# Moving the second group of row constants from the last y blocks to the place behind the first group

## The chip, the cores and the metric

The kernel runs on one NeuronCore of a Trainium2 chip. The metric is the device time of one execution in microseconds, the median over runs. The engines meant below are TensorE (PE; its weight loads are PEld), VectorE (DVE), ScalarE (ACT), GpSimd (POOL) and SyncE (SP). POOL and SP issue the DMA transfers: SP the plain ones, POOL the gathers and scatters by row number.

## The reference

The input is a matrix x of 2708 rows by 1024 columns and a 0/1 adjacency matrix of 2708 by 2708 with few ones in most rows. Two layers follow each other; each ends in a layernorm over the row.

```
q, k, v = x @ Wq.T + bq, x @ Wk.T + bk, x @ Wv.T + bv
z = (q @ k.T) / 32 * adj;  z = where(z == 0, -10000, z)
x1 = layernorm(x + relu(softmax(z, axis=1) @ v))
out = layernorm(x1 + adj @ (x1 @ W1) + b1)
```

Where a row of the adjacency matrix has any ones, only the columns with a one carry weight in the softmax. The kernel uses that: for each row it lists the columns with a one and works on those alone. A dense version follows in the program and is entered only if a check on the data fails.

## The kernel before, in words

The rows are handled in 22 blocks of 128 (`NB`; the last has 20 rows). Four pieces of work matter here.

**The y rows.** The score of rows i and j is rewritten as y_i . x_j plus a constant of row i, with y = x M + a bias row, and M made once from Wq and Wk. `y_block(b)` computes the block of y for the b-th 128 rows of x: two halves of 512 columns, each a chain of matmuls into one PSUM bank (L319), an add of the bias row by DVE that empties the bank (L323, raised in priority), and a write of the block to DRAM on SP's queue (L328). The next x block is loaded, transposed, on SP's queue (L280, three buffers `xt`). Along with it ACT sums the columns of x (L332).

**The row constants.** `row_constants(f)` makes the constant of each row, a dot product of the row of x with a vector `u_bc`. For each block it loads 128 rows of x into a tile `g` (L681, 512 KB, SP's queue), multiplies and sums in one DVE pass (L682), and at the end adds one number (L683) and writes the constants behind the y rows in DRAM (L684). Family 0 is row blocks 0 to 7 (eight passes), family 1 is blocks 8 to 20 (thirteen passes). The tiles `g` come from a pool of nine buffers (`G1 = 9`), which the attention gathers use as well, in the order in which they are asked for.

**The records.** Rows are sorted by their number of ones, and a record for each (its columns, its row number) is scattered to DRAM by POOL (L563) and read back into `tabs` (L568). `records_back(1, put)` turns the second family's records into masks on DVE (L593, L581, L582); its first step is told to stand behind `put`, the last DVE step of `row_constants(0)`.

**Attention and projection.** In the sorted order, a job of `attend` gathers 128 rows of y (`yg`, L343, two buffers) and for each slot 128 rows of x (`g`, L349), all on POOL's queue; takes a score for each slot with a DVE pass (L813, with L820 and L840 behind it), the exponentials on ACT (L849, L868) and sums the weighted rows with further DVE passes (L870) into `r`. Two jobs with many slots are worked in another form (`attend_shares`, L947). `flip` transposes `r` on PE (L716), ACT copies it out (L717) and `project` multiplies it by Wv (L739). `finish0` adds the bias (L906) and the gathered x row `xr`, and normalizes. The projection shares the four PSUM banks `po` with the y blocks.

The order is written out by hand: `steps` lists the y blocks 8 to 21 ("y"), the projections ("v") and later pairs of them ("p"), and a running credit decides in which step a job is started. Row blocks of records with family 1 can start only when all of y is written. A scheduler puts the instructions of each engine into one queue according to this order, their priorities and their dependences. [...]

In the kernel before, `row_constants(1)` is called in that loop, just ahead of `y_block(17)` (`b == NB - 5`), when family 1's y rows are still being computed.

Of the kernel before, what the change touches and what calls it, by code (L numbers as in the profile page):

```python
# [80 lines left out]
def sparse_part(ctx, tc, x, xT, adj, wqT, wkT, wvT, bq, bk, bv, w1, b1, out):  # L81
# [5 lines left out]
    NB = (N + P - 1) // P  # L87
# [23 lines left out]
    with es:  # L111
# [224 lines left out]
        def follow(later, earlier, same=False):  # L336

            kind = mybir.DependencyClass.NoSync if same else mybir.DependencyClass.Sync
            tc.add_manual_dep(later.ins, earlier.ins.name, mybir.DependencyInfo(kind, mybir.DependencyReason.DATA),
                              reason="an engine's queue shall not stand still for a transfer")  # L340
# [235 lines left out]
        def masks(ok, less_, d):  # L576

            shape = list(ok.shape)
            of = [places[:, :shape[-1]], d.to_broadcast(shape)] if len(shape) == 2 else \
                [places[:, :shape[2]].unsqueeze(1).to_broadcast(shape), d.unsqueeze(2).to_broadcast(shape)]  # L580
            put = nc.vector.tensor_tensor(ok, *of, op=ALU.is_lt)  # L581
            nc.vector.tensor_scalar(less_, ok, FAR, -FAR, op0=ALU.mult, op1=ALU.add)  # L582
            return put

        def records_back(f, behind=None):
            b0, nb = families[f]
            bs, js = slice(b0, b0 + nb), slice(0, max(SLOTS[max(b0, 1):b0 + nb]))
            if f == 0:
                deg0 = lists.tile([P, 1], F32, name="deg0")
                follow(nc.vector.tensor_copy(deg0, tab0[:, DEG:DEG + 1]), products[-1])  # L590
                nc.vector.tensor_scalar_add(deg0[:HUB], deg0[:HUB], float(-J0))
                masks(valid0, less0, deg0)
            put = nc.vector.tensor_copy(degs[:, bs], tabs[:, bs, DEG])  # L593
            follow(put, products[-1] if behind is None else behind, same=behind is not None)
            masks(valid[:, bs, js], less[:, bs, js], degs[:, bs])
# [69 lines left out]
        def g_tile():  # L665

            return gp.tile([P, D], F32, name="g", tag="g")
# [9 lines left out]
        def row_constants(f):  # L677
            b0, end = families[f][0], min(sum(families[f]), NB - 1)
            for b in range(b0, end):
                xg = g_tile()  # L680
                nc.sync.dma_start(out=xg, in_=x[b * P:(b + 1) * P])  # L681
                nc.vector.scalar_tensor_tensor(junkv, xg, 1.0, u_bc, op0=ALU.mult, op1=ALU.mult, accum_out=c_all[:, b, 0:1])  # L682
            put = nc.vector.tensor_scalar(c_all[:, b0:end, 0], c_all[:, b0:end, 0], y_bc[:, D:D + 1], None, op0=ALU.add)  # L683
            nc.sync.dma_start(out=y_ds[f][:(end - b0) * P, D:].rearrange("(b p) e -> p b e", p=P), in_=c_all[:, b0:end])  # L684
            return put

        put = row_constants(0)
        records_back(1, put)

        def gather(src, b, word, n):  # L690
            return gather_slot(src, tabs[:n, b, word:word + 1], n, g_tile())

        def gather_x(src, b):

            xr = wp.tile([P, D], F32, name="xr", bufs=3)
            return gather_at(src, tabs[:rows[b], b, ROW:ROW + 1], rows[b], xr)
# [280 lines left out]
        def turn_pair(flips, pool):  # L977

            A = []
            for k, flip_to in enumerate(flips):  # L980
                rT = (pool if k else wp).tile([P, DC, P], F32, name="rT", bufs=2)
                A.append(flip_to(rT))
            if len(flips) == 1:
                return A, None
            (a11, a12), (a21, a22) = [(a[:, :DC // 2], a[:, DC // 2:]) for a in A]
            s_all = wm_pool.tile([P, 4, DC // 2, P], F32, name="s_all", tag="m3")
            S = [s_all[:, i] for i in range(4)]
            nc.vector.tensor_add(S[0], a21, a22)
            nc.vector.tensor_sub(S[1], S[0], a11)
            nc.vector.tensor_sub(S[2], a11, a21)  # L990
            halves_turned.append(nc.vector.tensor_sub(S[3], a12, S[1]))
            return A, S

        def differences():
            return [wm_pool.tile([P, DC // 2, HALF], F32, name=f"t{k}", tag=f"m{k - 2}") for k in (2, 3, 4)]
# [97 lines left out]
        def blocks_of(step):  # L1093
            return [] if step[0] == "y" else [step[1]] if step[0] == "v" else list(step[1])
# [4 lines left out]
        def run_job():  # L1099

            b = jobs.pop(0)
            if b not in running:
                running[b] = (attend_one if b in single else attend_shares if b in (0, "hub") else attend)(b, got)
            next(running[b])
            J = HUB_SLOTS if b == "hub" else SLOTS[b]
            return 1.6 if b in single else SMALL + SLOT * J / len(pieces(J))

        def turn0(b):
            if b in last:
                rT = hp.tile([P, DC, HUB], F32, name="mean", tag="y0T")  # L1110
                nc.scalar.copy(rT, xbT.unsqueeze(2).to_broadcast([P, DC, HUB]))
                return rT
            return flip_shares([got["hub"], got[0]]) if b == 0 else flip(got[b])
# [5 lines left out]
        for i, (kind, b) in enumerate(steps):  # L1119
            if pending is not None:  # L1120
                pending[0](*pending[1:])
                credit -= END * (2 if pending[0] is finish_pair else 1)
                pending = None
            credit += STEP if kind != "p" else 2 * STEP - P_END
            step[0] = i
            for entry in joining[:]:
                if i >= entry[1] + 2:
                    entry[1] = i
                    next(running[entry[0]])
                    if entry[0] in got:  # L1130
                        joining.remove(entry)
            if kind == "p" and b == pairs[0]:

                (q11, q12), (q21, q22) = wv_q
                wv_t = differences()
                nc.vector.tensor_sub(q12, q12, q11)
                nc.vector.tensor_sub(wv_t[0], q22, q12)
                nc.vector.tensor_sub(wv_t[1], wv_t[0], q11)
                nc.vector.tensor_sub(wv_t[2], q21, wv_t[0])
            for c in [c for st in steps[i:i + 3] for c in blocks_of(st) if not (left_y and c in late)]:  # L1140
                while c not in done0 and c not in got and c != 0:
                    credit -= run_job()
            while 0 in jobs and i >= 15:
                credit -= run_job()
            while jobs and credit > 0 and len([c for c in got if c not in done0 and c not in ALONE and c != "hub"]) < (RB - 1 if left_y else RB):
                if left_y and len(jobs) <= late_jobs:
                    break
                credit -= run_job()
            for k, c in steps[i:i + 2]:
                if k != "y" and c not in turned and not (left_y and k == "p"):  # L1150
                    turned[c] = turn0(c) if k == "v" else turn_pair([lambda rT, r=got[b_]: flip(r, rT) for b_ in c], xb_pools[0])
                    done0.update(blocks_of((k, c)))
            if kind == "y":
                if b == NB - 5:
                    row_constants(1)
                y_block(b)
                credit -= Y_END
                left_y -= 1
                if left_y == 0:
                    xa.release()  # L1160
                    xb_pool = tc.alloc_tile_pool(name="xb", bufs=1, side="right", reuse_waits="tile")
                    xb_pools.append(xb_pool)
                    xb_bc.append(xb_pool.tile([P, D], F32, name="xb_bc"))
                    bcast_rows(xb_bc[0], xbT)
            elif kind == "v":
                xr = gather_x(x, b)
                pending = finish0, b, (project_mean if b in last else project)(turned[b], wv_q), xr
            else:
                for b_ in b:
                    pair_x[b_] = gather_x(x, b_)  # L1170
                pending = finish_pair, b, project_pair(b, *turned[b])
# [472 lines left out]
```

## Time and profile before

| | |
|---|---|
| median of 3 runs | 1066.83 us (1064.39, 1066.83, 1071.95) |
| profiled execution, span from first to last instruction | 1065.8 us |
| profiled execution, its own device time | not printed beside the span |
| PE busy | 1007.5 us (95%) |
| DVE busy | 850.6 us (80%) |
| POOL busy | 493.0 us (46%) |
| L682, one pass | 1.218 us median, 21 passes, from 250.5 to 486.7 us |
| L681, one load | 512 KB, 8.0 us median to landing |
| L349 gather of 128 rows of x | 1.0 us on POOL, 5.5 us median to landing |

A line of the profile's timeline gives the start in microseconds from the first instruction, the length, the engine, the line of the program, the operation, and what is written and read; in brackets stands how long the engine had been idle before it and whose event ended that. A line by stretch gives the busy time of each engine in it.

### The profile page before, as it was taken

How to read it: one execution, taken by the hardware profiler on the slowest of the kernel's cores; microseconds unless marked ns; L12 is line 12 of the kernel's file. 1: busy time of each engine (PE TensorE's matmuls, PEld its weight loads, DVE VectorE, ACT ScalarE, POOL GpSimd, SP SyncE). 2: the span in 40 equal slices, each digit the busy share in tenths (PEclk: the TensorE clock that was granted, in tenths of full speed). 3: DMA queues.
4: the chain of work that ended last, by engine and by line, in shares of the span. 5: the costliest groups of instructions: out<-in, count | busy, mean ns of one | idle time of the engine just before them, and what ended most of it. 6: DMA issues, size and time to landing. Idle time of an engine off the chain costs nothing.

```text
span 1065.8 us, 10216 instructions
## 1 busy us (share of the span) xinstructions
PE 1007.5 (95%) x2849; PEld 475.1 (45%) x2849; DVE 850.6 (80%) x1831; ACT 425.4 (40%) x894; POOL 493.0 (46%) x397
## 2 busy tenths in 40 slices
PE   7999999999988999999999999999589999999993
PEld 6444444444443444444545444444334444454441
DVE  8799999995287879999399999974678878896432
ACT  4688788422042332224424344332422363333321
POOL 1000140057654545526166666611577777787300
PEclk9999999999999999999999999999799999999997
DMA  9555458565887656796533777726589689979701
GB/s 363 184 205 204 167 207 290 160 216 168 292 250 253 200 181 203 236 331 201 175 114 96 239 247 258 260 95 210 151 286 262 201 274 324 282 221 323 192 40 42
DMA packets 90963, 229.20 MB, mean 215 GB/s; under 512 B 18411, under 2 KB 40395, under 8 KB 88189
## 3 DMA queue, kind: packets, MB, share of 16 engines
q0 software_dynamic: 48768, 148.05, 43.5%
q1 hardware_dynamic: 42128, 80.41, 21.9%
q8 instruction: 24, 0.39, 0.2%
q14 instruction: 43, 0.34, 0.1%
HBM read 219.61 MB, written 33.68 MB: 238 GB/s over the span
## 4 chain that ended last, share of the span: by engine, by line
PE 24%; DVE 12%; issue 5%; DMA 5%; POOL 3%; ACT 1%; POOLq 0%; DVEq 0%; ACTq 0%
PE po L999 21%; DVE r L870 3%; DMA g<-x_d,tabs 3%; DVE junkv L813 3%; DVE t L1011 1%; DMA yg<-y_d,tabs 1%; POOL g L349 1%; POOL xr L343 1%; PE tr L716 1%; PE po L739 1%; PE tr L729 1%; ACT junks L775 1%; DVE t L1069 1%; DVE r L1241 1%; DMA out_dram<-xr,tabs 0%
## 5 line engine op out<-in xcount | busy, mean ns | idle before, releaser
L319 PE MATMUL po<-m_sb,xt 128*128 128x512 f32 x672 | 292.1, 593 | 3.9 <-DVE yo L323 3.9
L319 PEld LDWEIGHTS po<-m_sb,xt 128*128 128x128 f32 x672 | 126.4, 190 | 160.1 <-issue 151.9
L813 DVE SCALAR_TENSOR_TENSOR junkv<-yg,g 128x1024 uint8<-128x1024 f32 x109 | 133.0, 1220 | 34.1 <-DMA g<-in_x_dram,tabs 16.7
L349 POOL DMA_INDIRECT g<-in_x_dram,tabs x86 | 110.7, 1288 | 72.3 <-DVE r L870 20.4
L999 PE MATMUL po<-t,s_all 128*128 128x512 f32 x272 | 124.3, 600 | 2.7 <-DVE xr L1011 2.7
L1241 DVE SCALAR_TENSOR_TENSOR r<-g,valid,r 128x1024 f32<-128x1024 f32 x77 | 98.6, 1281 | 19.1 <-DMA g<-x_d,tabs 18.3
L609 PE MATMUL po<-wk_o,wq_o 128*128 128x512 f32 x256 | 110.5, 592 | 0.0
L739 PE MATMUL po<-wv,rT 128*128 128x512 f32 x224 | 99.4, 602 | 3.6 <-DVE pr L855 3.0
L775 ACT ACTIVATE junks<-t,lnm 128x1024 uint8<-128x1024 f32 (+1 forms) x41 | 47.0, 1147 | 123.7 <-DVE lnm L773 95.2
L349 POOL DMA_INDIRECT g<-x_d,tabs x67 | 77.6, 1158 | 22.7 <-issue 12.8
L563 POOL DMA_INDIRECT tab_d<-rec,pos_i x22 | 27.1, 1230 | 130.0 <-DVE pos_i L552 123.6
L870 DVE SCALAR_TENSOR_TENSOR r<-g,pr,r 128x1024 f32<-128x1024 f32 x64 | 81.8, 1279 | 5.9 <-ACT r L882 4.6
L999 PE MATMUL po<-w,rT 128*128 128x512 f32 x192 | 86.4, 599 | 0.0
L332 ACT ACTIVATE junka<-xt 128x128 f32<-128x128 f32 x176 | 53.8, 306 | 76.1 <-PE po L319 57.5
L999 PEld LDWEIGHTS po<-t,s_all 128*128 128x128 f32 x272 | 51.9, 192 | 68.5 <-issue 61.9
L788 ACT ACTIVATE t<-t,nmr,rstd 128x1024 f32<-128x1024 f32 (+1 forms) x41 | 50.0, 1237 | 81.2 <-DVE nmr L787 81.0
L224 DVE MAX8 few<-a 128x8 f32<-128x75 f32 (+3 forms) x132 | 79.2, 618 | 0.0
L609 PEld LDWEIGHTS po<-wk_o,wq_o 128*128 128x128 f32 x256 | 48.3, 190 | 59.3 <-issue 59.1
L999 PE MATMUL po<-w,s_all 128*128 128x512 f32 x160 | 72.1, 592 | 0.0
L221 DVE SCALAR_TENSOR_TENSOR a<-a,iota 128x2708 f32<-128x2708 f32 (+1 forms) x22 | 65.2, 2963 | 5.4 <-ACT junk L220 5.4
L739 PEld LDWEIGHTS po<-wv,rT 128*128 128x128 f32 x224 | 42.8, 193 | 57.6 <-issue 56.8
L717 ACT COPY rT<-tr 128x512 f32<-128x512 f32 x80 | 43.1, 586 | 56.1 <-PE tr L716 56.1
(350 smaller groups left out, 1524.6 us busy)
## 6 DMA issues: line engine op xcount, KB each, us to landing
a<-in_adj_dram SPq DMA_DIRECT2D x21, 1354.0 KB, 5.9
xt<-in_xT_dram SPq DMA_DIRECT2D x21, 512.0 KB, 5.2
y_d<-yo SPq DMA_DIRECT2D x21, 512.0 KB, 6.1
g<-in_x_dram SPq DMA_DIRECT2D x21, 512.0 KB, 8.0
wq_i<-in_wqT_dram SPq DMA_DIRECT2D x8, 512.0 KB, 8.7
wk_i<-in_wkT_dram SPq DMA_DIRECT2D x8, 512.0 KB, 10.9
wv<-in_wvT_dram SPq DMA_DIRECT2D x16, 256.0 KB, 6.0
w<-in_w_dram SPq DMA_DIRECT2D x4, 1024.0 KB, 7.8
```

The costliest lines, as they stand in the source:

```text
L221: nc.vector.scalar_tensor_tensor(a[:n], a[:n], 1.0, iota[:n], op0=ALU.is_equal, op1=ALU.mult)
L224: nc.vector.max(few[:n, i * 8:(i + 1) * 8], a[:n, cuts[i]:cuts[i + 1]])
L319: put = nc.tensor.matmul(po, xt[:, c, :], m_sb[c // 2][:, c % 2, k0:k1], start=(c == 0), stop=(c == DC - 1))
L332: put = nc.scalar.activation(junka, xts[b][:, c, :], AF.Copy, accum_out=xs[:, c, b:b + 1])
L349: nc.gpsimd.indirect_dma_start(out=dst[:n], out_offset=None, in_=src, in_offset=bass.IndirectOffsetOnAxis(ap=at, axis=0), bounds_check=N - ...
L609: nc.tensor.matmul(po, wq_o[i // 2][:, o, i % 2 * P:(i % 2 + 1) * P], wk_o[:, o, hs], start=(o == 0), stop=(o == DC - 1))
L739: put = nc.tensor.matmul(acc, rT[:, c, :], w[c // 4][h][:, c % 4, :], start=(c == 0), stop=(c == DC - 1))
L775: nc.scalar.activation(junks[:n], t[:n], AF.Square, bias=nm[:n], accum_out=vs[:n])
L813: nc.vector.scalar_tensor_tensor(junkv[:n], yg[:n, :D], scale, xg[:n], op0=ALU.mult, op1=ALU.mult, accum_out=s)
L870: nc.vector.scalar_tensor_tensor(r[:n], xg[j][:n], pr[:n, j:j + 1], r[:n], op0=ALU.mult, op1=ALU.add)
L999: put = nc.tensor.matmul(acc, a[:, k], w[:, k], start=start and k == 0, stop=stop and k == DC // 2 - 1, skip_group_check=True)
L1241: put = nc.vector.scalar_tensor_tensor(r[:n], xg[:n], ok[:n, j:j + 1], r[:n], op0=ALU.mult, op1=ALU.add)
```

## The change

The call `row_constants(1)` is taken out of the loop over the steps and put directly behind `row_constants(0)` and `records_back(1, put)`, ahead of all attention jobs. It issues the same instructions: thirteen loads on SP's queue, thirteen DVE passes, one DVE add and one write. The thirteen tiles `g` are now asked for ahead of those of the first attention job. Lines behind the new call have a number that is one higher in the changed kernel up to the loop.

```diff
         put = row_constants(0)
         records_back(1, put)
+        row_constants(1)
...
             if kind == "y":
-                if b == NB - 5:
-                    row_constants(1)
                 y_block(b)
                 credit -= Y_END
                 left_y -= 1
```

## The prediction

> **What bounds the kernel now.** I read the page's busy shares first, then the busy time by stretch, then the queues of the vector engine (DVE) and of TensorE (PE) in order of time around the two places that the change touches, then PE's waits.
>
> ```profile
> span 1065.8 us, 10216 instructions
> PE 1007.5 (95%) x2849; PEld 475.1 (45%) x2849; DVE 850.6 (80%) x1831; ACT 425.4 (40%) x894; POOL 493.0 (46%) x397
> ```
>
> PE is busy 95%, so the 58 us in which it stands still are where time can be won or lost. By stretch (columns: length, then busy time of PE, PEld, DVE, ACT and POOL, clock, DMA share, GB/s), the place that the work leaves:
>
> ```profile
> 440.00:480.00 40.00, 40.00 (x95) 17.73 (x94) 38.66 (x64) 8.64 (x33) 14.18 (x11) 1.00 0.82 286
> 480.00:520.00 40.00, 40.00 (x152) 18.14 (x151) 31.35 (x68) 14.34 (x64) 18.40 (x15) 1.00 0.66 209
> ```
>
> PE has no gap there, though DVE is full until 510. The place that the work goes to is DVE's queue between 261 and 288:
>
> ```profile
> 261.62 0.23 DVE L683 TENSOR_SCALAR c_all<-c_all,y_bc 128x8 f32<-128x8 f32 x1
> 274.32 0.23 DVE L593 CAST degs<-tabs 128x14 f32<-128x14 int32 x1 [12.46 <-DMA tabs<-tab_d]
> 275.50 0.68 DVE L323 TENSOR_TENSOR yo<-po,y_bc 128x512 f32<-128x512 f32 x1
> 287.58 1.23 DVE L813 SCALAR_TENSOR_TENSOR junkv<-yg,g 128x1024 uint8<-128x1024 f32 x1 [11.41 <-DMA yg<-y_d,tabs]
> ```
>
> Two holes: 12.5 us until the second family's records are back, 11.4 us until the first row of y is gathered for attention. Behind the second, PE pays, because the adds that empty its four PSUM banks (L323) queue behind attention:
>
> ```profile
> 293.47 7.13 PE L319 MATMUL po<-m_sb,xt 128*128 128x512 f32 x16 [1.44 <-DVE yo L323]
> 301.55 7.13 PE L319 MATMUL po<-m_sb,xt 128*128 128x512 f32 x16 [0.95 <-DVE yo L323]
> 309.22 7.13 PE L319 MATMUL po<-m_sb,xt 128*128 128x512 f32 x16 [0.53 <-DVE yo L323]
> 318.16 14.04 PE L319 MATMUL po<-m_sb,xt 128*128 128x512 f32 x32 [0.93 <-DVE yo L323]
> 335.23 10.09 PE L739 MATMUL po<-wv,rT 128*128 128x512 f32 x19 [3.03 <-DVE pr L855]
> ```
>
> Together 6.9 us of PE stall. After 335 PE does not stop again until 524. The last y block ends at 523; its write and the late attention jobs hang on that, so whatever PE is early or late at 523 reaches the end of the kernel one for one.
>
> [...] the add of 292.73 stood behind the wait of 11.4 us although its matmuls had ended near 271 (halves of 6.9 us, counted back from 292.0). [...] L682 has a median of 1.218 us here.
>
> **The change, part by part.**
>
> *Removed at 453 to 488.* Thirteen L682 passes at a pitch of 1.27 us (253.55, 254.81, 256.08 in the first group) are 16.5 us of DVE, with 13 loads of 512 KB, one small add and one small write on SP. Direct worth: nothing, as PE covers it (80.0 of 80 us busy). DVE simply reaches its idle time earlier; from 509 to 523 it already stands still but for a few adds, waiting for PE and for a write of y. In the new order attention scores stand where the first L682 stood, so the adds near 464 are not freed; the relief starts near 478.
>
> *Added after 274.* In the built order of the changed kernel the copy of the records (L593) stays ahead of the 13 passes, so the first hole stays and only the second is used. Records arrive at 273.1 (the tabs load is issued 1.2 us earlier on POOL, since one gather no longer stands ahead of it). Then 13 x 1.27 = 16.5, the masks 1.2 and the two adds of block 8 1.2 us: DVE is free at 273.1 + 18.9, about 292.3 with the small add. Attention begins 292.5 against 287.6: it is 4.9 us late.
>
> *Moved on POOL.* In the built order the three xr gathers and the first two yg gathers come ahead of all g gathers. These g gathers need the buffers of the 5th to 13th pass: 281, 283, 284 and so on, with 6 us to land. The first three are there by 290, before DVE is free. From then on gather and pass form one loop over nine buffers (a pass frees a buffer, a gather of about 6 us fills it), which in the kernel before cost DVE 8.6 us of waiting from 300 to 345. I walked it pass by pass with 1.27 us passes and 6 us gathers. The waits come again: the first scores of row blocks 4, 3 and 2 start at 304.8, 317.6 and 333.7 against 299.7, 311.7 and 327.5, and block 2's last maximum is taken at 358.4 against 353.2. So the lag, call it d, is 5.2.
>
> *Moved on SP.* Five loads stand ahead of one xt load, seven ahead of the next; the seven wait for the first passes, so that xt goes out near 280 and not 271.5. It is used near 299: covered by some 14 us. If that cover is gone, PE waits for it.
>
> *What PE gains first.* The adds now stand ahead of attention or early in it. Block 8's second half is added at 287 (before 292.7), block 9's halves at 294 and 302 (before 300.8 and 308.5), block 11's at 324 and 333.6. PE needs those banks at 292, 299, 306, 327 and 334. All are in time, so the 6.9 us of stalls go.
>
> *What is late next.* PE is now up to 6.9 us early and DVE d late, and the banks' slack between them is finite. In the kernel before, the tightest are those of block 17:
>
> ```profile
> 457.26 0.68 DVE L323 TENSOR_TENSOR yo<-po,y_bc 128x512 f32<-128x512 f32 x1
> 464.20 0.68 DVE L323 TENSOR_TENSOR yo<-po,y_bc 128x512 f32<-128x512 f32 x1
> 464.10 13.90 PE L319 MATMUL po<-m_sb,xt 128*128 128x512 f32 x32
> ```
>
> The first bank is free at 457.9 and taken at 464.1, the second at 464.8 and 471.0: slack 6.2 both times (others have 7.1 to 13). PE can therefore be early by 6.2 - d at most, and every further microsecond of d makes it late. DVE does not wait for PE between 345 and 460, so nothing there works d off.
>
> *How large d is.* With 5.2 the gain is 1.0 us. Two things add to it that the trace does not price. Eight of the 13 loads (4.2 MB) now go out at 251 to 263, together with the 14 scatters of the records and ahead of their reading back; the DMA shares there are 0.72, 0.29, 0.62 and 0.17 per 5 us, so at some 400 GB/s (measured 285 to 290) the 10.5 us of traffic just fit, but a scatter or the reading back can be 0 to 5 us later. I take 2. And the scores that replace L682 near 464 need gathered rows: 0 to 2, I take 0.5. So d = 7.7 and the loss is 1.5 us. Bounds: d = 0 if the loop's waits swallow the lag (gain 6.2); d = 17 if DVE's hole is of no use (loss 10.8).
>
> The sum: 1065.8 + 1.5 in the span. The page prints no other time of that execution; its span is 1.0 below the median of the three runs, so I add the 1.5 to the median 1066.8: **1068.3 us**.
>
> **Rivals.**
> - *A, forecast:* the lag and the slack nearly cancel, d from 4.5 to 10: 1065 to 1071. [...] Chance 0.55.
> - *B, the lag is absorbed:* the waits for gathers in the kernel before (3.2 us at 332 and 365, 4.1 at 381) would be shorter when DVE comes later; with d of 0 to 2 PE keeps 4 to 6 us: 1061 to 1063. Against it: POOL itself waits for DVE to free buffers (26.9 us on r L870). Chance 0.19.
> - *C, slower:* the loads of x and the scatters collide, the records come back 5 to 10 us late, and since L593 is first in DVE's queue all 13 passes stand behind it. d is 12 to 17: 1073 to 1078. It decides from d = 6.2 on, and costs over 1% from d = 16.9. For it: the 21 loads landed after anything from 3.8 to 11.1 us. Against it: half-empty DMA from 255 to 270. Chance 0.22.
> - *D, other:* work after 523 falls differently, either way by up to 12 us. 0.04.
>
> **The numbers.** The likeliest is A. Range 1061 to 1077, from B's gain to nearly all of C. One per cent, 10.7 us, is about what a measurement of this kernel can tell from no change. Faster by more needs more stall than PE has before 335: 0.03. Slower by more is the upper end of C and part of D: 0.16. Within: 0.81.
>
> **What the changed profile should show.** L593 still ends a long wait, at 273 to 277, and 13 L682 follow it. The first L813 is near 292 to 296. The stalls of PE behind L323 and L739 between 290 and 336 are gone or below 2 us in sum. Stalls of 1 to 3 us appear between 345 and 465, behind L323 or the adds L906 (each line one lower down in the changed file). DVE is idle for some 15 us more between 490 and 523. The last y block ends within 3 us of 523. I am wrong if L593 comes after 280, if PE stays early by 4 us or more at 450, or if PE stalls in the first rows of attention after all.

## The result and the profile after

The changed kernel takes 1082.14 us (median of 4 runs, 1080.40 to 1085.92), the kernel before 1065.61 (4 runs): 1.0145 times as long, with a 95% interval of 1.0117 to 1.0172. (The ratio is as recorded; the two medians alone give 1.0155. Ratios below are as recorded too.) The forecast was 1068.3 with a range up to 1077. The medians lie 16.5 us apart, and the range does not hold that. The profiled execution took 1080.40 us.

The head of the page of the changed kernel, and its busy time by stretch (columns as above):

```profile
span 1078.6 us, 10213 instructions
PE 1011.3 (94%) x2849; PEld 475.4 (44%) x2849; DVE 851.6 (79%) x1831; ACT 424.9 (39%) x894; POOL 496.2 (46%) x397
```

```profile
440.00:480.00 40.00, 40.00 (x101) 18.18 (x100) 37.98 (x66) 10.97 (x37) 21.19 (x16) 1.00 0.71 224
480.00:520.00 40.00, 40.00 (x98) 17.95 (x97) 25.08 (x50) 14.14 (x66) 15.72 (x13) 1.00 0.54 168
```

At the old place nothing is won or lost, as forecast: PE is full in both stretches, and DVE has 25 us of work, not 31, in the second. At the new place, DVE's queue:

```profile
278.24 0.17 DVE L593 CAST degs<-tabs 128x14 f32<-128x14 int32 x1 [15.89 <-DMA tabs<-tab_d]
...
296.11 1.22 DVE L814 SCALAR_TENSOR_TENSOR junkv<-yg,g 128x1024 uint8<-128x1024 f32 x1
```

The first hole has grown from 12.46 to 15.89 us, the second is filled, and attention begins at 296.11, not 287.58: 8.5 us late. PE's queue from there to 446 (the stretch without a gap before 302 left out):

```profile
302.06 15.67 PE L319 MATMUL po<-m_sb,xt 128*128 128x512 f32 x32 [2.79 <-DMA xt<-in_xT_dram]
...
333.36 7.13 PE L740 MATMUL po<-wv,rT 128*128 128x512 f32 x16 [1.02 <-ACT rT L718]
...
349.61 7.13 PE L319 MATMUL po<-m_sb,xt 128*128 128x512 f32 x16 [0.80 <-DVE yo L323]
358.76 7.13 PE L319 MATMUL po<-m_sb,xt 128*128 128x512 f32 x16 [2.01 <-DVE yo L323]
366.49 14.00 PE L740 MATMUL po<-wv,rT 128*128 128x512 f32 x32 [0.59 <-ACT rT L718]
...
429.70 15.62 PE L740 MATMUL po<-wv,rT 128*128 128x512 f32 x32 [6.10 <-ACT rT L718]
```

The load of the xt block that PE needs at 302.06 had gone out at 284.00; the share of the DMA engines is 0.98 to 1.05 from 280 to 305, and in the kernel before only from 275 to 290. PE is 1.9 us early at 333 and 1.2 us late at 366. Then, at the projection of row block 3 (called v3 from here), it waits 6.10 us. The kernel before had no wait there:

```profile
422.03 13.90 PE L739 MATMUL po<-wv,rT 128*128 128x512 f32 x32
```

The matmuls behind the wait take 15.62 us instead of 13.90. The wait is for ACT's copy of the turned rows. ACT's queue at that place, in the kernel before and in the changed one:

```profile
417.65 0.30 ACT L940 ACTIVATE pr<-scores,nm 128x5 f32<-128x5 f32 x1 [16.16 <-DVE nm L931]
...
419.12 1.05 ACT L717 COPY rT<-tr 128x512 f32<-128x512 f32 x2
```

```profile
427.61 0.30 ACT L941 ACTIVATE pr<-scores,nm 128x5 f32<-128x5 f32 x1 [16.03 <-DVE nm L932]
...
429.08 1.05 ACT L718 COPY rT<-tr 128x512 f32<-128x512 f32 x2
```

The copies had their data since 408.5 and 409.9, when PE ended the transposes. They stand behind the first exponentials of the hub job (one of the two jobs with many slots, L940), and these wait 16 us for a maximum (nm) from DVE. In both traces the two copies, 1.05 us of work, ran only after them: some 11 us after their data had come in the kernel before, and 19 us in the changed one. So a late DVE reaches PE through a third engine. DVE takes the maximum, in the kernel before and in the changed one:

```profile
417.46 0.15 DVE L931 TENSOR_REDUCE nm<-scores 128x1 f32<-128x5 f32 x1
```

```profile
427.42 0.15 DVE L932 TENSOR_REDUCE nm<-scores 128x1 f32<-128x5 f32 x1
```

It is 9.96 us late there.

Up to the end of the y blocks the sum closes. PE begins v3 2.28 us after that maximum (429.70 - 427.42). In the kernel before that would have been 419.74, but PE came only at 422.03: a slack of 2.29 us. With 9.96 us of lag PE is 9.96 - 2.29 = 7.67 us late (measured: 429.70 - 422.03 = 7.67), the slower matmuls add 15.62 - 13.90 = 1.72, and the end of the last y block moves from 523.23 to 532.63, which is 9.40.

The slower matmuls are the clock. Granted clock (the column before the last two) of the changed kernel around the wait:

```profile
420.00:424.00 4.00, 3.60 (x9) 1.33 (x7) 3.15 (x5) 0.00 (x0) 1.28 (x2) 1.00 0.83 265
424.00:430.00 6.00, 0.30 (x1) 0.30 (x2) 6.00 (x11) 2.36 (x5) 4.15 (x3) 0.68 0.46 129
430.00:434.00 4.00, 4.00 (x7) 1.59 (x6) 4.00 (x6) 1.83 (x6) 3.46 (x2) 0.63 0.49 151
434.00:438.00 4.00, 4.00 (x11) 1.85 (x10) 4.00 (x9) 1.85 (x12) 2.93 (x3) 1.00 0.74 209
```

The clock was 0.68 in the stretch that holds the wait, 0.63 behind it and 1.00 again from 434. The price was 1.72 us here, and 1.7 to 2.8 in the runs below. Some shorter waits cost it too: the 32 matmuls behind the 2.79 us at 302.06 took 15.67 us, with a clock of 0.50 from 304 to 306.

The records are late because their scatters are. POOL's reading back of the records, in the kernel before and in the changed one:

```profile
268.96 1.17 POOL L568 DMA_DIRECT2D tabs<-tab_d  x1
```

```profile
274.17 1.16 POOL L568 DMA_DIRECT2D tabs<-tab_d  x1 [7.47 <-DMA tab_d<-rec,pos_i]
```

In the changed kernel it waits 7.47 us for the 14 scatters. Those issued between 250 and 275, with the median time to landing in us at the end of the line, before and changed:

```profile
tab_d<-rec,pos_i POOLq DMA_INDIRECT x13, 2.8
```

```profile
tab_d<-rec,pos_i POOLq DMA_INDIRECT x13, 6.2
```

Of the 16.5 us between the medians, 9.4 are there at the end of the y blocks, and 12.8 in the spans of the two profiled executions (that of the changed kernel was the shortest of its four). The remaining 3.4 us of the spans lie after 800 us, in code that the change does not touch, and 3.7 among the executions. So 7.1 of the 16.5 us are not explained here.

### The profile page after: what moved, and what is told of

Its sections match the earlier page's. It is cut to its first block, busy times and chain, and to the rows that moved or that the text cites. A ratio compares the mean times of both kernels' runs of the same rounds, so it can differ in the third digit from the quotient of the medians.

```text
span 1078.6 us, 10213 instructions
## 1 busy us (share of the span) xinstructions
PE 1011.3 (94%) x2849; PEld 475.4 (44%) x2849; DVE 851.6 (79%) x1831; ACT 424.9 (39%) x894; POOL 496.2 (46%) x397
## 5 line engine op out<-in xcount | busy, mean ns | idle before, releaser
L349 POOL DMA_INDIRECT g<-in_x_dram,tabs x86 | 113.6, 1320 | 67.3 <-ACT r L869 18.8
L349 POOL DMA_INDIRECT g<-x_d,tabs x67 | 81.5, 1217 | 22.7 <-issue 14.3
L219 ACT ACTIVATE junk<-a 128x2708 uint8<-128x2708 f32 (+1 forms) x22 | 54.1, 2458 | 25.0 <-DMA a<-in_adj_dram 20.4
```

What stands on the lines that cost most here:

```text
L219: nc.scalar.activation(junk[:n], a[:n], AF.Sign, accum_out=cnt[:n, b:b + 1])
L349: nc.gpsimd.indirect_dma_start(out=dst[:n], out_offset=None, in_=src, in_offset=bass.IndirectOffsetOnAxis(ap=at, axis=0), bounds_check=N - ...
```

## The experiments

My theory: (a) the loads of x at the new place delay the scatters and so the records; (b) the 13 passes stand behind them on DVE and add their time; (c) the lag is paid by PE at v3, through ACT's queue; (d) with a slower clock behind the long wait. Rivals: the loads alone cost, or the passes alone; the banks are the only limit, as forecast; ACT's order is only where the lag shows.

The experiments fell on six chips, and ratios are to the kernel before on the same chip. On some PE ran through from 238 to 290 as in the traces above (the kernel before took 1066 to 1069 us there). On others it stood still for 5 to 10 us between 258 and 276, in every trace, that of the kernel before included (it took 1079 to 1082 us). I call them chips with the stop. Each of the six was used for one group of runs, and the four with the stop came one after the other, so whether the stop belongs to the chip or to the time is open.

**Half of the change each, and two other orders.** On a chip with the stop. Only the passes, without their loads (and without their tiles of the pool):

```diff
-                xg = g_tile()
-                nc.sync.dma_start(out=xg, in_=x[b * P:(b + 1) * P])
+                xg = g_tile() if f == 0 else u_bc
+                if f == 0:
+                    nc.sync.dma_start(out=xg, in_=x[b * P:(b + 1) * P])
```

> The 13 passes stand at their new place but read u_bc, which is on chip, in place of rows of x: their 13 loads are gone, and with them the rows' constants of the second family are left out of the computation. Theory (records late by the loads, passes behind the records, lag paid at ScalarE's queue in v3): with no loads the records' copy comes at 273 to 275 as in the kernel before, attention begins at 291 to 293, DVE runs 4 to 6 us late at 400, PE waits 2 to 4 us for v3's rT copy near 420 and reaches the end of the y blocks 2 to 4 us later than before: 1067 to 1070 us. Rival 1 (the passes are covered, the loads alone cost): within 1 us of before, 1065 to 1067. Rival 2 (the prediction's bank slack of 6.2 us is the only limit): PE 1 us early, 1063 to 1065.

Only the loads, with passes of 8 columns:

```diff
-                nc.vector.scalar_tensor_tensor(junkv, xg, 1.0, u_bc, op0=ALU.mult, op1=ALU.mult, accum_out=c_all[:, b, 0:1])
+                w = D if f == 0 else 8
+                nc.vector.scalar_tensor_tensor(junkv[:, :w], xg[:, :w], 1.0, u_bc[:, :w], op0=ALU.mult, op1=ALU.mult, accum_out=c_all[:, b, 0:1])
```

> The 13 loads of x stand at their new place, but each pass multiplies 8 columns, not 1024; the rest of the dot product of the second family's constants is left out. Theory: the records' copy comes at 277 to 279, as in the changed kernel, attention begins at 290 to 293 (the gathers start as late as the records), DVE is 3 to 6 us late at 400, v3 waits 1 to 4 us, and the run takes 1066 to 1070 us; so neither half alone gives the 16.5 us of the change, because each lag by itself is mostly eaten by the 2 us of slack at v3 and by the stalls that go before 336. Rival 1 (the loads alone cost): 1075 to 1083. Rival 3 (the loads are free, the passes cost): 1063 to 1066.

Six passes early, seven at the old place (`row_constants` takes the first and last block):

```diff
-        row_constants(1)
+        row_constants(1, end=FAMILY + 6)
...
             if kind == "y":
+                if b == NB - 5:
+                    row_constants(1, b0=FAMILY + 6)
```

> Six of the 13 passes with their loads at the new place, seven at the old one; everything is computed. Theory: the six loads that go out ahead of the scatters are still there, so the records come at 276 to 278; six passes, masks and an add take 9.5 us behind them, attention begins at 287 to 290, d is 1 to 3 us, v3 waits under 1.5 us, and the run takes 1063 to 1068 us. Rival (the cost is proportional to the passes moved, 1.27 us each): half of 16.5, 1073 to 1075.

All passes ahead of the records' copy on DVE:

```diff
         put = row_constants(0)
+        put = row_constants(1)
         records_back(1, put)
-        row_constants(1)
```

> All 13 passes at the new place but ordered ahead of the records' copy, so that DVE works them off in the first hole, as their rows land; everything is computed. Theory: the loads (6.8 MB at some 290 GB/s) keep the passes going until 277 to 282, the records' copy follows, attention begins at 284 to 289, d is -3 to 2 us, v3 does not wait, and the stalls of PE before 336 are halved or gone: 1060 to 1066 us, 15 to 21 us under the changed kernel. Rival 3 (passes cost wherever they stand near 280): within 4 us of the changed kernel. Rival 1 (loads alone cost): within 4 us of the changed kernel too.

Measured: pass_only 1.0133 (1.0091 to 1.0174), load_only 1.0100 (1.0055 to 1.0144), split_6_7 1.0057 (1.0022 to 1.0092), passes_first 1.0149 (1.0100 to 1.0197). All four expected times missed, on the slow side. In split_6_7 PE does not wait at v3, as expected, but its time lies near that of its rival, a cost in proportion to the passes moved. Its trace does not show where it lost: the y blocks end 0.4 us after those of the kernel before with the stop (before_again, on another chip). The stop could have come from these edits, so the kernel before was traced too.

> The kernel before, unchanged, for a trace on the chip of these runs. In the four runs so far PE stood still for some 12 us between 258 and 273 [...], while the runs of the kernel before on that chip took 1078.6 us, 13 more than on the first chip. If the stop belongs to the chip, it is in this trace too, and the time is near 1078; if it belongs to the edits, PE runs through from 238 to 292.

> The same kernel as pass_only: the 13 passes read what is on chip, no loads; the constants of the second family are left out. Without the stop of PE at 258 the theory's numbers stand: the records' copy at 273 to 275, attention at 291 to 293, DVE 4 to 6 us late at 400, a wait of 2 to 4 us at v3 for the rT copy, 2 to 4 us slower than before. With the stop: the records are there before DVE is, and the lag is set by the stop plus the passes.

The stop is in before_again too (1084.51 us in one run). DVE's queue there:

```profile
275.50 0.69 DVE L323 TENSOR_TENSOR yo<-po,y_bc 128x512 f32<-128x512 f32 x1 [21.51 <-remote]
...
284.32 0.17 DVE L593 CAST degs<-tabs 128x14 f32<-128x14 int32 x1
...
297.02 1.23 DVE L813 SCALAR_TENSOR_TENSOR junkv<-yg,g 128x1024 uint8<-128x1024 f32 x1 [11.07 <-DMA yg<-y_d,tabs]
```

With the stop DVE waits 21.51 us for PE's matmuls at an add (the view gives "remote"), so that the first hole does not exist and the records are there before DVE is. The passes then cost DVE 5.2 us (first score at 302.26 in pass_only_again), and PE waited 6.52 us at v3; the run took 1.0069 (1.0032 to 1.0106). In pass_only, where 2 to 4 us at v3 were expected, it had waited 5.90.

**The two halves where PE runs through.** On a chip without the stop:

> The same kernel as pass_only (13 passes over what is on chip; the second family's constants are left out). If PE runs through: records' copy at 273 to 275, attention at 291 to 293, the hub job's first maximum 4 to 6 us later than 417.46, and so v3 begins 2 to 4 us later than 422.03. If PE stops: a repeat of the two runs so far, 1.007 to 1.013 of before.

> The same kernel as load_only (13 loads, passes of 8 columns; the rest of the dot product of the second family's constants is left out). If PE runs through at 258 to 274 as in the first two traces: the records' copy comes near 278 and DVE then stands for the rows of x themselves; if the loads alone make DVE late, the hub job's first maximum comes 4 to 8 us later than 417.46 and PE waits for it at v3; if only passes do, PE does not wait there. If PE stops: a repeat of load_only, 1.006 to 1.014 of before.

Passes alone: 1.0067 (1.0046 to 1.0088). Loads alone: 1.0139 (1.0099 to 1.0179). DVE's queue of load_only_2, POOL's, and v3 on PE:

```profile
277.76 0.17 DVE L593 CAST degs<-tabs 128x14 f32<-128x14 int32 x1 [16.29 <-DMA tabs<-tab_d]
285.10 0.17 DVE L683 SCALAR_TENSOR_TENSOR junkv<-g,u_bc 128x8 uint8<-128x8 f32 x1 [4.63 <-DMA g<-in_x_dram]
```

```profile
273.89 1.15 POOL L568 DMA_DIRECT2D tabs<-tab_d  x1 [8.08 <-DMA tab_d<-rec,pos_i]
```

```profile
427.67 15.79 PE L741 MATMUL po<-wv,rT 128*128 128x512 f32 x32 [5.24 <-ACT rT L719]
```

And pass_only_3, the same three places:

```profile
273.65 0.29 DVE L593 CAST degs<-tabs 128x14 f32<-128x14 int32 x1 [11.87 <-DMA tabs<-tab_d]
...
291.52 1.22 DVE L815 SCALAR_TENSOR_TENSOR junkv<-yg,g 128x1024 uint8<-128x1024 f32 x1
```

```profile
268.87 1.17 POOL L568 DMA_DIRECT2D tabs<-tab_d  x1
```

```profile
428.82 16.48 PE L741 MATMUL po<-wv,rT 128*128 128x512 f32 x32 [6.28 <-ACT rT L719]
```

Part (a) is shown where PE runs through: with the loads POOL waits 8.08 us for the scatters and the records' copy comes at 277.76; without them it waits for nothing and the copy comes at 273.65, as in the kernel before. With the stop POOL waits at most 1.5 us for the scatters; there DVE waits for the rows of x themselves, 16.7 us in load_only, and the changed kernel still takes 1.0092 and 1.0156 (below). Part (b) is shown too: passes alone put attention at 291.52, 3.9 us late. What I had wrong is that the halves would each be small: in pass_only_3 copy and first score came as expected, but the maximum 9.1 us late where 4 to 6 had been expected, and v3 6.8 us late, not 2 to 4. The loads alone hold DVE without the stop too, beyond the late records, because it waits for the rows (11.2 us in four waits of L683 in load_only_2), and either half alone makes PE wait over 5 us at v3. So neither rival ("the loads alone", "the passes alone") stands, and the halves do not add up: 0.0067 + 0.0139 is more than the whole. The loads bring the thirteen tiles of the pool with them; what these cost the gathers by themselves was not tested.

**Is it ACT's queue?** The changed kernel again, and with one order turned: the hub job's first exponentials behind v3's copies.

```diff
-                nc.scalar.copy(rT[:, g * 4:g * 4 + 4, :], tr)
+                put = nc.scalar.copy(rT[:, g * 4:g * 4 + 4, :], tr)
+            copies.append(put)
             return rT
...
-                nc.scalar.activation(pr[:, :m], z, AF.Exp, bias=nm, accum_out=den)
+                put = nc.scalar.activation(pr[:, :m], z, AF.Exp, bias=nm, accum_out=den)
+                if b == "hub" and i == 0:
+                    follow(put, copies[3], same=True)
```

> The changed kernel, unchanged, on the chip of these runs. If PE stops at 258 to 274 here too, DVE sits at its add of block 8 until 275, works off the first group and the records' copy comes near 284 with no wait of its own; 13 passes, masks and adds (17.9 us in pass_only_again) then put the start of attention at 302 against 297.0 in before_again, and the theory expects PE to wait 5 to 8 us at v3 for the rT copy behind the hub job's exponentials: 1.01 to 1.016 of before. If PE does not stop: as in the first trace, 1.0145.

> The changed kernel with one order turned round on ScalarE: the hub job's first exponentials stand behind v3's rT copies, not ahead of them; nothing is computed otherwise. Theory: PE's wait at v3 (5 to 8 us) goes, DVE's lag of 8 to 10 us stays and meets the next limit, the four banks, with 6.2 us of slack at block 17, so that the y blocks end 3 to 6 us earlier than in after_again: 1.003 to 1.009 of before. Rival (ScalarE's order is a symptom; the lag is paid wherever PE next needs DVE): PE waits as long behind an add or a copy within the next 30 us, and the time is within 2 us of after_again.

> The kernel before with the same turn on ScalarE. PE does not wait at v3 there (slack 2.0 us in the first trace), so the theory expects no gain: within 3 us of before.

> The changed kernel, unchanged, beside the next run on one chip, to size the noise: its traces so far have waits of 6.1 and 6.4 us at v3, ends of the y blocks at 532.6 and 539.7, and 546 to 547 us from there to the end; so 1.01 to 1.018 of before.

> The same kernel as hub_behind. Its times lay 6 us under after_again, but its trace ended the y blocks at 539.60, where after_again has 539.69: PE took v3 3.8 us earlier and gave that back in seven waits of 0.4 to 1.6 us behind DVE between 455 and 494. If the turn on ScalarE is worth its 6 us, this run is 5 to 7 us under after_third and its y blocks end that much earlier after the start of attention; if DVE's lag is paid wherever PE needs DVE next, within 3 us of after_third, and the y blocks end as late.

> The same kernel as hub_behind: the changed kernel with v3's rT copies ahead of the hub job's exponentials on ScalarE. Two pairs so far put it 6.3 and 1.6 us under the changed kernel. Where PE runs through: v3 begins near 424, not 429.70; with a lag of 10 us and 6.2 us of slack in the banks at block 17 PE then waits some 4 us between 440 and 500, so that the y blocks end near 527 to 529, not 532.63: 1.006 to 1.010 of before. Rival (all of it is given back): y blocks at 531 or later, 1.012 to 1.016.

The changed kernel repeats with the stop: after_again 1.0156 (1.0115 to 1.0197) and after_third 1.0092 (1.0058 to 1.0125), with waits of 6.44 and 6.13 us at v3. With the turn: hub_behind 1.0049 (1.0025 to 1.0072), hub_behind_2 1.0058 (1.0032 to 1.0084), and on a chip without the stop hub_behind_3 1.0088 (1.0062 to 1.0114), where the changed kernel had 1.0145 in its own comparison. All three lie under the changed kernel, by 6.3 and 1.6 us where both ran on one chip. The traces show what becomes of the released time. PE in hub_behind, v3 and four of the waits from 446 to 495:

```profile
433.00 13.90 PE L743 MATMUL po<-wv,rT 128*128 128x512 f32 x32
...
455.10 7.13 PE L319 MATMUL po<-m_sb,xt 128*128 128x512 f32 x16 [0.47 <-DVE yo L323]
463.81 7.10 PE L743 MATMUL po<-wv,rT 128*128 128x512 f32 x16 [1.57 <-DVE t L910]
471.74 7.13 PE L743 MATMUL po<-wv,rT 128*128 128x512 f32 x16 [0.82 <-DVE nm L935]
479.64 14.02 PE L319 MATMUL po<-m_sb,xt 128*128 128x512 f32 x32 [0.77 <-DVE yo L323]
```

v3 begins without a wait, 3.8 us earlier than in after_again, but the matmuls of 494.21 follow instead of those of 494.41, and the y blocks end at 539.60 instead of 539.69: in this trace all is given back behind DVE, most of it at the banks, as the rival had it. In hub_behind_2 the maximum came 5.8 us later than in after_third, and the y blocks ended at 542.40, 3.6 us after those of after_third. In hub_behind_3 v3 begins at 423.94, as expected, but then PE waits for the add of a projection's bias (t), and the 32 matmuls behind that wait take 15.52 us, not 13.90:

```profile
455.34 15.52 PE L743 MATMUL po<-wv,rT 128*128 128x512 f32 x32 [2.38 <-DVE t L910]
```

Its y blocks end at 530.82, where 527 to 529 had been expected and 531 or later from the rival; that is 1.8 us before those of the changed kernel's first trace. So ACT's order sets the place where the lag is paid. That it sets the price is not shown: if it is turned, the banks take most of the same lag in each of the three traces, and what makes the medians lower stays open. hub_behind_before (1.0104, 1.0052 to 1.0155, four runs) was expected within 3 us of before and was not. Its trace has no stall at v3, but PE waits 3.38 us at 527 for the last xt load, and the 64 matmuls behind that take 5.32 us (3.67 in before).

**The lag in all traces.** First score, the hub job's first maximum on DVE, start of v3 on PE, its wait there, and the end of the y blocks, in us from the start of each trace. With the stop, PE stood still for 5.7 to 10.1 us in these traces, so rows of that part differ by the stop as well:

| run | first score | maximum | v3 | wait | y end | ratio |
|---|---|---|---|---|---|---|
| *PE runs through* | | | | | | |
| before | 287.58 | 417.46 | 422.03 | 0 | 523.23 | 1 |
| pass_only_3 | 291.52 | 426.54 | 428.82 | 6.28 | 532.60 | 1.0067 |
| load_only_2 | 293.22 | 425.38 | 427.67 | 5.24 | 530.77 | 1.0139 |
| passes_first_2 | 291.49 | 424.22 | 426.51 | 6.22 | 529.91 | 1.0066 |
| changed | 296.11 | 427.42 | 429.70 | 6.10 | 532.63 | 1.0145 |
| *with the stop* | | | | | | |
| before_again | 297.02 | 426.99 | 430.07 | 0 | 532.78 | 1 |
| split_6_7 | 298.81 | 429.59 | 431.88 | 0 | 533.19 | 1.0057 |
| after_third | 300.25 | 433.27 | 435.55 | 6.13 | 538.82 | 1.0092 |
| passes_first | 300.76 | 433.77 | 436.05 | 6.39 | 540.09 | 1.0149 |
| after_again | 301.56 | 434.50 | 436.78 | 6.44 | 539.69 | 1.0156 |
| load_only | 301.69 | 433.66 | 435.95 | 5.85 | 539.09 | 1.0100 |
| pass_only_again | 302.26 | 436.31 | 438.59 | 6.52 | 542.02 | 1.0069 |
| pass_only | 303.27 | 435.06 | 437.35 | 5.90 | 540.80 | 1.0133 |

In each row with a wait, v3 begins 2.28 or 2.29 us after the maximum. split_6_7 is on the edge: its v3 starts 2.29 us after the maximum and PE comes just then. Part (c) stands on this as to the place: for kernels with different loads, passes and orders, one number on DVE gives PE's start. Part (d) too: behind these ten waits 32 matmuls took 15.60 to 16.73 us, and 13.90 in the rows before and before_again; in split_6_7 they took 14.00. The granted clock was read behind two of the waits: 0.63 from 430 to 434 in the changed kernel, 0.51 from 438 to 443 in pass_only_again. The ratios scatter more than the ends of the y blocks do; the time from there to the end is 542.5 to 557.8 us, for the kernel before alone 542.5 and 550.0.

Between the first score and the maximum the lag grows: from 8.5 to 10.0 us in the changed kernel, from 3.9 to 9.1 in pass_only_3. In that stretch DVE waits for gathered rows (without those of the hub job) 16.7 us in the kernel before, 18.0 in the changed one and 20.8 in pass_only_3. What makes these waits longer, I did not isolate.

**Two attempts to win.** The passes ahead of the records, where the hole exists:

> The same kernel as passes_first: all 13 passes ahead of the records' copy. Where PE runs through at 258 to 274, DVE has a hole of 12 to 16 us for them, as their rows land (11 MB from 245 at some 400 GB/s: the last near 275 to 280); attention begins at 285 to 291, the hub job's first maximum 0 to 4 us later than 417.46, v3 waits under 2 us: 0.996 to 1.004 of before. Rival (the traffic alone makes DVE late, as in load_only_2): attention at 293 or later, a wait of 4 us or more at v3, 1.008 to 1.015. Where PE stops: a repeat of 1.0149.

It took 1.0066 (1.0046 to 1.0087): better than the changed kernel, slower than before. The waits of PE between 280 and 345 are gone, all of them. But the DMA moved 302 GB/s from 250 to 275, not some 400, POOL waits 7.01 us for the scatters, attention begins 3.9 us late, and v3 waits 6.22 us. The rival's numbers are nearer than mine.

From the kernel before, the adds of blocks 8 and 9 ahead of the first score, with the turn on ACT:

```diff
+                    adds.append(nc.vector.tensor_add(yo[:n, k0:k1], po[:n], y_bc[:n, k0:k1]))
...
+            if not scores_:
+                follow(put, adds[-1], same=True)
+            scores_.append(put)
...
+            if i == 1 and 1:
+                y_block(b)
```

> Made from the kernel before: the four adds of blocks 8 and 9 stand ahead of the first score on DVE (they cost 2.4 us in a hole of 11 us there), and v3's rT copies ahead of the hub job's exponentials on ScalarE; the second group of constants stays at its old place. Theory (what costs is DVE's order against PE's banks, not the amount of work): PE's first stalls at 290 to 330 shrink by up to 6 us on a chip where PE runs through at 260, by up to 3.5 us where it stops there, and the run is 0 to 6 us faster than before. Rival (PE regains nothing, since DVE's attention ends as late and PE waits for it at v6, which took 3.03 us in the first trace): within 2 us of before.

It took 1.0079 (1.0047 to 1.0110). PE has no stall from 280 to 345 (3.6 us in before_again) and reaches v3 4.2 us earlier, at 425.91. By 514.2 the lead is gone (before_again is at 513.5 there), mostly in waits for DVE from 455 to 494. Then PE waits 5.29 us for the last load of xt, where before_again waits 1.44:

```profile
455.95 7.11 PE L743 MATMUL po<-wv,rT 128*128 128x512 f32 x16 [1.53 <-DVE t L913]
...
528.01 5.20 PE L306 MATMUL po<-m_sb,xt 128*32 128x257 f32 x64 [5.29 <-DMA xt<-in_xT_dram]
```

SP had issued that load at 521.49; in the first trace of the kernel before it goes out at 506.85 and PE takes it at 513.51 without a wait. The load is for the block of 20 rows, whose tile POOL clears first:

```profile
520.49 0.97 POOL L279 MEMSET xt<- 128x1024 f32 x1
```

That step stands behind gathers. In the first trace of the kernel before, the first of them waited 5.37 us for DVE (it began at 501.31); in adds_first POOL was busy for 0.52 us from 510 to 515. So here too DVE seems to reach PE through another queue, POOL's; the 3.38 us of hub_behind_before end with the same load. A gain at 290 is lost from 455 on. No version beat the kernel before.

## Why the prediction was wrong

*Removed at 453 to 488, worth nothing:* held. PE is full there in both kernels.

*Added after 274:* the order was right (copy first, then 13 passes), and the price nearly so: 17.9 us from the copy to the first score, 19.4 allowed. (The sum rests on the measured pitch of 1.27 us a pass.) The copy's time was wrong: 278.24, not 273.1. This is the step "How large d is", where a scatter or the reading back was allowed to be 0 to 5 us late and 2 was taken. It was 5.1. The DMA share from 255 to 270, 0.36 in the kernel before, was read as room for 4.2 MB; with the loads it was 1.04. POOL waits for the last of 14 small scatters, and these landed after a median of 6.2 us, not 2.8; the average share before had not shown that. Rival C named exactly this collision.

*Moved on POOL, the loop carries the lag:* wrong in size. I walked the loop and found the same lag at its end. It grew by 1.4 us in the changed kernel and by 5.1 in pass_only_3. So d was 9.96 at the maximum, not 7.7.

*Moved on SP, covered by some 14 us:* failed. The load went out at 284.00, 4 us later than taken, and PE waited for an xt load until 302.06, 2.79 us. I had allowed no more than the seven buffers' time for it.

*What PE gains first, 6.9 us:* only in part. The stalls on adds between 290 and 336 did go, but xt and a copy cost 3.8 us there and the clock behind the xt wait 1.8, and by 366 PE was 1.2 us late.

*What is late next:* this is the step that failed. It listed the slack of the PSUM banks, found 6.2 us at block 17, and took that as the only way from DVE to PE. The way with the least slack ran over ACT, with 2.29 us at v3. With the forecast's own d of 7.7 this slack gives 5.4 us and the slower clock behind the wait, not 1.5. With the measured d it gives the 9.4 us of the y phase to 0.01 us. The lower clock behind a long wait was in no step at all. From the forecast's 1.5 us to the 9.4 at the end of the y blocks, 3.9 come from the slack, 2.3 from d and 1.7 from the clock. The slack of the banks was too wide as well: in hub_behind_3, where the way over ACT is free, the maximum is 10.2 us late, which leaves 4.0 us by the forecast's slack, and the y blocks end 7.6 us late.

*The decision point of rival C* was put at d = 6.2 and its time at 1073 to 1078; with 2.29 in place of 6.2 it gives 1076 at d = 10 with the clock. The rest, up to 1082, lies behind the y blocks and among the executions, and stays open.

Of what the changed profile was to show, the passes behind the copy came, and the start of attention just past its late end of 296, by some luck, since a copy 5.1 us late and a price 1.5 us too high partly cancel; DVE's idle time came smaller (4.9 us more from 490 to 523, where some 15 were forecast). The copy at 278.24 lies just outside 273 to 277. A stall "of 1 to 3 us behind L323 or the adds" came as one of 6 us behind a copy, and the last y block ended 9.4 us late, not within 3.

## What to carry to other kernels

When an engine is made late, list every queue in which something for the bottleneck stands behind something of the late engine, not only the buffers that the two share: here the tightest was a copy on a third engine, ready for 19 us, behind an exponential of another job. Then ask what the next tightest queue takes: with that copy moved ahead, PE paid most of the lag at its banks, and in another version at a load that stood behind POOL. Price a stall of the tensor engine with the slower matmuls that follow it: 1.7 to 2.8 us here, behind waits of 5.2 to 6.5 us. And before bulk loads are put next to small scatters that others wait for, look at what the last scatter's landing releases: a mean DMA share of 0.36 from 255 to 270 in the kernel before did not keep the scatters of the changed one from taking a median of 6.2 us to land, not 2.8.

## What the runs showed of the hardware that I had not expected

On the chips with the stop, PE issues single matmuls mostly 1.4 to 3.5 us apart between 260 and 275, waiting for nothing that the trace shows. The busy time by stretch of before_again:

```profile
255.00:260.00 5.00, 5.00 (x13) 2.09 (x11) 0.00 (x0) 0.00 (x0) 3.83 (x4) 1.00 0.19 68
260.00:275.00 15.00, 6.72 (x8) 1.94 (x8) 0.00 (x0) 0.80 (x4) 10.00 (x10) 0.67 0.44 133
```

DVE does nothing for the whole of it. It is in each of the traces of those chips at the same place of the program, and in none of the other chips. What holds PE there is open. The kernel before is some 13 us slower where it happens.

After the waits of 5.2 to 6.5 us at v3 each of the ten groups of matmuls was slower. At v6, the projection near 340, a shorter wait does not show it every time: behind 3.03 us in the first trace of the kernel before 32 matmuls took 15.67 us, with a clock of 0.70 from 335 to 339; behind 3.06 us in before_again they took 13.97. So of these two waits near 3 us one cost time and one did not, and the ten of 5.2 us or more at v3 all did.
